# Graph attention: turned one-hots by comparing the edges' rows, queries spread by one fp32 product a chunk

## The chip, the cores and the metric

The kernel runs on one core of one Trainium2 chip. The metric is the device time of one execution in microseconds (us); the time shown for a kernel is the median of its runs. A core has five engines with queues of their own: TensorE (PE) for matrix products, VectorE (DVE), ScalarE (ACT), GpSimd (POOL), and SyncE (SP), which here only issues DMAs. PE keeps one operand of a product still (it is loaded by its own instruction, shown as PEld) [...].

## The reference, cut to what matters

A graph of 3125 nodes with 256 features and 53125 edges (25000 random ones in both directions and a loop at each node, sorted by target node) goes through eight layers in turn: graph attention, a small mixture of experts, a three-layer graph convolution, a second mixture of experts, and so on. Every layer adds its result to `x`. The change is in the first layer, the attention, which computes, for 8 heads of 32 features (`SCALING` is 32 to the power -0.5):

```python
def _L0_gnn_ref(nfeat, attn_bias, Wq, Wk, Wv, Wo, src, dst):    # nfeat = layernorm(x)
    q = (nfeat @ Wq.T).reshape(n, HEADS, HEAD_DIM) / SCALING
    k = (nfeat @ Wk.T).reshape(n, HEADS, HEAD_DIM)
    v = (nfeat @ Wv.T).reshape(n, HEADS, HEAD_DIM)
    attn = jnp.einsum('ehd,ehd->eh', k[src], q[dst])
    attn = attn + attn_bias
    m = jax.ops.segment_max(attn, dst, num_segments=n)
    a = jnp.exp(attn - m[dst])
    s = jax.ops.segment_sum(a, dst, num_segments=n)
    a = a / s[dst]
    out = jax.ops.segment_sum(v[src] * a[:, :, None], dst, num_segments=n)
    return out.reshape(n, FEAT) @ Wo.T
```

So each edge needs the query of its target node (`dst`) and the key and value of its source node (`src`).

## The kernel before, in words

Nodes are cut into T = 25 tiles of P = 125. Since edges are sorted by target, the edges of a tile are one stretch of at most 18 chunks of 128 edges (WC = 18), handled in three parts of PC = 6 chunks. In what follows "tile" is one of the 25.

Setup (`edges_in`, L1735 on) reads the edges by windows, turns them with PE so that an edge has a partition, and leaves `row_w`, the place of each edge's target in its tile, as bf16 (L1755). At the same time keys and values of all nodes are computed and stored to DRAM (`kv_d`), the normalized rows as well (`lt_d`), and the edges' attributes (`eb_d`).

Then comes the loop over tiles. For a tile:

- `one_hot` builds on DVE a matrix `oh` with edges on partitions and a 1 in the column of the edge's target (L282, in bf16); it also issues, on SP, the loads of `lt_t` (L1804) and `eb_t` (L1806).
- `one_hot_turned` transposes `oh` chunk by chunk on PE (L1826, 18 times) and copies the result from PSUM to `oht` by ACT (L1827, three times).
- `queries` computes the tile's queries with two fp32 products (L266, which is the line of the helper `product`) and splits them into three bf16 terms whose sum holds them in full (L1815 to L1819: ACT, DVE, DVE, ACT, DVE in a chain).
- `logits`, once a part, gathers the part's keys and values by POOL's indirect DMAs (`kv`, L1660, six of 256 KB), spreads the queries to the edges by three bf16 products a chunk with `oht` as the still operand (`qx`, L1840), multiplies them into the keys on DVE (L1843, two chunks at a time) and sums per head (L1844). `qx` has two buffers in PSUM.
- `sums_of` makes the exponentials and sums them per target by PE (L1850 to L1858); `weights_of` spreads the sums' logarithms to the edges with `oht` (L1868) and makes the weights.
- `weighted` multiplies the values by the weights (L1878), casts `oh` to fp32 on ACT (L1883) and sums over edges by fp32 products (`acc`, L1885).
- `normed`, `normed_turned` and `projected` divide, transpose (L1902) and multiply by `wo` (L266), and add to `x` (L1909).

The loop is pipelined over three tiles: an iteration computes the logits of tile t (`now`), weights and sums those of tile t-1 (`before`), and prepares tile t+1 (`after`). Between these pieces `beside()` issues one step of the next layer, the experts of two tiles at a time (L770 to L893), and each iteration from the sixth on ends with a step of `Windows` (L1974 on), which prepares a later stage and whose small loads come every fifth tile. The order of the instructions on each engine isn't the order of the text: a planner orders them when the kernel is built, by the order of the text as priority, by its own costs, and by when buffers come free. At run time every engine, and SP's DMA issue, follows that order and waits in it.

Buffers: `kv` has seven, most of the others two. They come from the pool `att_t` (`tiles` in the code), which was laid out before setup's pool.

Of the kernel before, what the change touches and what calls it, by code (L numbers as in the profile page):

```python
# [10 lines left out]
F32 = mybir.dt.float32  # L11
F32R = mybir.dt.float32r
I32 = mybir.dt.int32
BF16 = mybir.dt.bfloat16
AF = mybir.ActivationFunctionType
# [7 lines left out]
N, D = 3125, 256  # L23
# [47 lines left out]
def gnn_ffn_kernel(ctx: ExitStack, tc: tile.TileContext, a, out: bass.AP):  # L71
# [1555 lines left out]
    def attention(windows, experts):  # L1627
# [6 lines left out]
        eb_d = dram.tile([128, T, H, WC], F32, name="eb_d")  # L1634
        win_d = dram.tile([T * WC], I32, name="win_d")
        KO, VO, AO = 16, 16 + D, 7
        WB = T * WC // 5
        with ExitStack() as es:
# [50 lines left out]
            first = big.tile([1, T + 1], F32, name="first")  # L1689
            at = pool.tile([WB, 5], I32, name="win_at", bufs=1)  # L1690

            def begins():
# [42 lines left out]
            def edges_in():  # L1735
# [11 lines left out]
                for ws, to in zip(got, (src_f, dst_f)):  # L1747
                    for b, w in enumerate(ws):
                        wf = pool.tile([WB, 128], F32, name="wf")
                        nc.vector.tensor_copy(wf, w)  # L1750
                        turned(to[:, b * WB:(b + 1) * WB].rearrange("p (t c) -> p t c", t=5), wf)
                    if to is src_f:
                        nc.vector.tensor_copy(src_i, src_f)
                    else:
                        nc.vector.tensor_sub(row_h, twice(dst_f), twice(base.rearrange("p t c -> p (t c)")))  # L1755
                    yield
# [32 lines left out]

            pool = tiles  # L1790
            psum = es.enter_context(tc.tile_pool(name="ps_att", bufs=3, space=PSUM, reuse_waits="tile"))
# [4 lines left out]

            def one_hot(t):
                s = Tile()
                s.t, s.kv = t, begun if t == 0 else []
                oh = pool.tile([128, WC, HC], BF16, name="oh")  # L1800
                one_hots(oh, row_h[:, t * WC:(t + 1) * WC, :], iota_h)
                s.oh = oh[:, :, :P]
                s.lt = pool.tile([128, 2, P], F32, name="lt_t")
                nc.sync.dma_start(s.lt, lt_d[:, :, t, :].rearrange("k f p -> f k p"))  # L1804
                s.eb = pool.tile([128, H, WC], F32, name="eb_t")
                nc.sync.dma_start(s.eb, eb_d[:, t])  # L1806
                return s

            def queries(s):

                ps = psum.tile([P, D], F32, name="sm")
                product(ps, [(s.lt[:, k, :], wq[:, k, :]) for k in range(2)])
                s.q = pool.tile([P, 3, D], BF16, name="q_t")
                q = pool.tile([P, D], F32, name="q")
                nc.scalar.activation(q, ps, AF.Copy, scale=float(HD) ** 0.5)  # L1815
                nc.vector.tensor_copy(s.q[:, 0, :], q)
                nc.vector.tensor_sub(q, q, s.q[:, 0, :])
                nc.scalar.copy(s.q[:, 1, :], q)
                nc.vector.tensor_sub(s.q[:, 2, :], q, s.q[:, 1, :])  # L1819

            def one_hot_turned(s):
                s.oht = pool.tile([P, WC, 128], BF16, name="oht")
                for c0 in range(0, WC, PC):
                    ps = psum.tile([128, 1024], BF16, name="sm")
                    for c in range(PC):
                        nc.tensor.transpose(ps[:P, c * 128:(c + 1) * 128], s.oh[:, c0 + c, :], ident_h)  # L1826
                    nc.scalar.copy(s.oht[:, c0:c0 + PC, :].rearrange("d c e -> d (c e)"),  # L1827
                                   ps[:P, :PC * 128])
                s.l = pool.tile([128, WC, H], F32, name="l")

            def logits(s, p):
# [4 lines left out]
                for c0 in range(0, PC, 2):  # L1836
                    ps = psum.tile([128, 2, D], F32, name="qx", bufs=2)
                    for c in range(2):
                        for k in range(3):
                            nc.tensor.matmul(ps[:, c, :], s.oht[:, p * PC + c0 + c, :], s.q[:, k, :],  # L1840
                                             start=(k == 0), stop=(k == 2))
                    k_ = kv[:, c0:c0 + 2, KO:VO]
                    nc.vector.tensor_mul(k_, k_, ps)  # L1843
# [45 lines left out]
            def normed(s):  # L1889
# [3 lines left out]
                nc.vector.reciprocal(inv, inv)  # L1893
                s.ao = pool.tile([P, D], F32, name="ao")
                nc.vector.tensor_mul(s.ao.rearrange("p (h d) -> p h d", h=H),
# [3 lines left out]
            def normed_turned(s):  # L1899
                ps = psum.tile([128, 2, P], F32, name="sm")  # L1900
                for k in range(2):
                    nc.tensor.transpose(ps[:, k, :], s.ao[:, k * 128:(k + 1) * 128], ident[:P, :P])  # L1902
                s.at = pool.tile([128, 2, P], F32, name="at")
                nc.scalar.copy(s.at, ps)
# [5 lines left out]

            now, before = one_hot(0), None
            one_hot_turned(now)
            queries(now)
            more = experts()
            for t in range(T + 1):
                def beside():
                    more.step(t - 1)

                if now:
                    logits(now, 0)  # L1920
# [5 lines left out]
                beside()  # L1926
                after = one_hot(t + 1) if t + 1 < T else None
                if before:
# [590 lines left out]
```

## Time and profile before

| | us |
|---|---|
| median of 3 runs | 3410.41 |
| lowest, highest | 3407.14, 3412.61 |
| profiled execution, its own time | 3415.6 |
| its span in the profile | 3413.8 |
| first and last qx product | 119.7, 892.4 |
| PE busy | 3132.9 (92%) |
| DVE busy | 1742.2 (51%) |
| ACT busy | 1034.0 (30%) |
| POOL busy | 680.0 (20%) |

The profile is of one execution. Busy time is the time in which at least one instruction of the engine is under way; a matmul's length holds the time that it takes to come out, so the start-to-start distance of several in a row (their pitch) is the better measure of what one costs. "Idle before" is idle time of the engine just ahead of an instruction, and the name behind `<-` is what ended it. The granted clock is the share of TensorE's full clock, as a mean over a stretch. Lines (L1840) are those of the kernel.

### The profile page before, as it was taken

The numbers are of one execution on the slowest core, as the hardware profiler recorded it, in microseconds if no ns is written. First come the engines' busy times: TensorE is split into PE (matmuls) and PEld (weight loads), VectorE is DVE, ScalarE is ACT, GpSimd is POOL, SyncE is SP. The second block draws the span as 40 slices with busy tenths as digits, with TensorE's granted clock in tenths as the row PEclk, the third lists the DMA queues.
The fourth block names the chain that finished last, engine by engine and source line by source line (L and its number), as shares of the span: only waits on it lengthen the run. The fifth ranks groups of instructions, "written<-read, shape, count | busy, mean of one in ns | idle before, by whom it ended". The sixth has DMA issues, their size and how long they took to land. (4 is left out here: it accounts for less than half of the span.)

```text
span 3413.8 us, 45380 instructions
## 1 busy us (share of the span) xinstructions
PE 3132.9 (92%) x16587; PEld 2446.2 (72%) x16587; DVE 1742.2 (51%) x4905; ACT 1034.0 (30%) x1996; POOL 680.0 (20%) x639
## 2 busy tenths in 40 slices
PE   6688998998888899999996999979999999999898
PEld 2466776777677789898885888868755555579666
DVE  6577778777697534344674122155521111355662
ACT  1222332332255423232331222234423232332120
POOL 1665564655100000000134333200000000000000
PEclk9789998999889999999997999989999999999997
DMA  5755554555256734444344666553200000043001
GB/s 165 235 172 150 160 163 143 160 165 144 61 165 215 192 99 119 102 108 110 91 123 133 185 178 180 167 137 103 69 19 10 10 19 10 7 122 100 21 1 39
DMA packets 253208, 388.23 MB, mean 114 GB/s; under 512 B 41454, under 2 KB 201069, under 8 KB 252973
## 3 DMA queue, kind: packets, MB, share of 16 engines
q1 hardware_dynamic: 184090, 226.68, 23.3%
q0 software_dynamic: 54064, 141.25, 15.3%
q10 hardware_dynamic: 14819, 17.27, 1.9%
q8 instruction: 134, 2.20, 0.3%
q14 instruction: 101, 0.83, 0.1%
HBM read 314.47 MB, written 70.58 MB: 113 GB/s over the span
## 5 line engine op out<-in xcount | busy, mean ns | idle before, releaser
L2222 PE MATMUL agg<-cnt_f,hp 125*128 125x500 f32 (+1 forms) x3500 | 733.1, 369 | 22.2 <-ACT hp L2163 22.0
L2222 PEld LDWEIGHTS agg<-cnt_f,hp 125*128 125x128 f32 x3500 | 635.5, 189 | 103.2 <-ACT hp L2163 23.1
L1660 POOL DMA_INDIRECT kv<-kv_d,src_w x450 | 450.9, 1002 | 281.5 <-PE acc L1885 140.5
L2200 ACT CAST cnt_f<-blk 125x500 fp32r<-125x500 bf16 (+1 forms) x435 | 245.5, 565 | 518.4 <-PE agg L2222 496.7
L2200 DVE CAST cnt_f<-blk 125x500 fp32r<-125x500 bf16 (+1 forms) x440 | 185.5, 423 | 265.5 <-PE agg L2222 221.6
L1382 DVE SCALAR_TENSOR_TENSOR x<-po,gall,x 125x256 f32<-125x256 f32 x200 | 93.8, 484 | 417.5 <-PE po L266 416.9
L1376 ACT ACTIVATE h<-hid_ps,shift,scale 128x500 f32<-128x500 f32 (+1 forms) x224 | 161.9, 723 | 376.0 <-PE hid_ps L266 375.5
L1840 PE MATMUL qx<-q_t,oht 125*128 125x256 bf16 x1350 | 216.2, 296 | 53.9 <-DVE kv L1843 41.2
L1885 PE MATMUL acc<-kv,oh_f 128*125 128x265 f32 x900 | 224.9, 412 | 14.6 <-DVE kv L1878 14.6
L1885 PEld LDWEIGHTS acc<-kv,oh_f 128*125 128x125 f32 x900 | 178.5, 201 | 54.2 <-DVE kv L1878 18.5
L1840 PEld LDWEIGHTS <-oht 125*128 125x128 bf16 x1350 | 138.2, 105 | 100.4 <-issue 50.6
L266 PE MATMUL po<-wslot,h 128*125 128x256 f32 x800 | 203.0, 386 | 0.1
L266 PEld LDWEIGHTS po<-wslot,h 128*125 128x125 f32 x800 | 145.0, 187 | 75.2 <-ACT h L1376 27.0
L266 PE MATMUL hid_ps<-h,wslot 128*128 128x500 f32 (+1 forms) x448 | 193.8, 556 | 4.1 <-ACT h L1376 0.6
L266 PE MATMUL hid_ps<-xe,wslot 128*128 128x256 f32 x832 | 187.3, 383 | 1.8 <-DVE xe L1214 1.8
L1072 POOL DMA_INDIRECT xs_d<-r_l,pos x50 | 60.2, 1204 | 645.3 <-DVE r_l L1068 567.1
L266 PE MATMUL hid_ps<-v_rows,wslot 128*128 128x500 f32 (+1 forms) x448 | 186.8, 537 | 0.0
L1225 ACT ACTIVATE hid<-hid_ps,wslot 128x256 f32<-128x256 f32 x208 | 98.5, 475 | 286.8 <-PE hid_ps L266 286.8
L266 PE MATMUL po<-wslot,hid 128*128 128x256 f32 x832 | 184.5, 378 | 0.0
L266 PEld LDWEIGHTS hid_ps<-xe,wslot 128*128 128x128 f32 x832 | 150.7, 191 | 33.4 <-ACT hid L1225 4.1
L266 PEld LDWEIGHTS po<-wslot,hid 128*128 128x128 f32 x832 | 155.7, 189 | 21.8
L1843 DVE TENSOR_TENSOR kv<-kv,qx 128x512 f32<-128x512 f32 x225 | 150.7, 679 | 26.2 <-PE qx L1840 24.7
(512 smaller groups left out, 4625.8 us busy)
## 6 DMA issues: line engine op xcount, KB each, us to landing
wslot<-in_ex_W SPq DMA_DIRECT2D x52, 1024.0 KB
blk<-an_d SPq DMA_DIRECT2D x60, 546.9 KB
blk<-at_d SPq DMA_DIRECT2D x40, 546.9 KB
blk<-an_d SPq DMA_DIRECT2D x45, 410.2 KB
at_d<-ab SPq DMA_DIRECT2D x25, 683.6 KB
an_d<-an SPq DMA_DIRECT2D x25, 683.6 KB
blk<-at_d SPq DMA_DIRECT2D x30, 410.2 KB
kv<-kv_d,src_w POOLq DMA_INDIRECT x450, 3.7
```

The source lines that it names most:

```text
L266: nc.tensor.matmul(ps, l, r, start=(bias is None and i == 0), stop=(i == last))
L1072: st = nc.gpsimd.indirect_dma_start(out=xs_d, in_=l2[:, i, :].bitcast(I32), in_offset=None, out_offset=bass.IndirectOffsetOnAxis(ap=self.p ...
L1225: nc.scalar.activation(hid[:, m, :], ps[:, :BLK], AF.Gelu, bias=c[:, 4 + m:5 + m])
L1376: nc.scalar.activation(dst[:, m, :c], ps[:, :c], AF.Relu, bias=shift[:, l, col:col + 1], scale=scale[:, l, col:col + 1])
L1382: nc.vector.scalar_tensor_tensor(x[:, t0 + i, :], po, gating.all[:, t0 + i, e:e + 1], x[:, t0 + i, :], ALU.mult, ALU.add)
L1660: got = nc.gpsimd.indirect_dma_start(out=kv[:, c, KO:], out_offset=None, in_=kv_d, in_offset=bass.IndirectOffsetOnAxis(ap=src_i[:, at + c: ...
L1840: nc.tensor.matmul(ps[:, c, :], s.oht[:, p * PC + c0 + c, :], s.q[:, k, :], start=(k == 0), stop=(k == 2))
L1843: nc.vector.tensor_mul(k_, k_, ps)
L1885: nc.tensor.matmul(s.acc[:, :D + H + 1], of[:, c, :], kv[:, c, AO:VO], start=(p == 0 and c == 0), stop=(p == 2 and c == PC - 1))
L2200: to(f[:, :n, :], part[0][:, :n, m % MB, :])
L2222: nc.tensor.matmul(ps[f][:, :c], hp[:, m, k, f * 128:(f + 1) * 128], got[:, :c], start=(m == 0 and k == 0), stop=(m == T - 1 and k == 1))
```

## The change

The transposed one-hots are no longer made by transposing. Setup writes the edges' places in their tiles, one row of 128 for each chunk, to a DRAM tensor `turned_d` (five subtractions and five stores). For each tile a load repeats its 18 rows, 4608 bytes, on all 125 partitions; DVE then compares in place with the partition's own number, which gives `oht` directly. The load is issued by a new function `asked`, together with the loads of `lt_t` and `eb_t`, and `asked` for tile t+1 stands at the head of iteration t. ACT casts `oht` to fp32, a part at a time, into `oht_f` with three buffers.

Queries stay in fp32 as they come from PSUM, without the split, and are spread by one fp32 product a chunk.

The tiles of the loop move from `att_t` to a new pool, `att_s`, which is laid out where setup's pool was; `ao` and `at` have one buffer instead of two.

```diff
+        turned_d = dram.tile([T * WC, 128], BF16, name="turned_d")
...
+            first_row = pool.tile([WB, 1], F32, name="first_row", bufs=1)
+            nc.vector.memset(first_row, 0.0)
+            for k in range(1, 5):
+                nc.vector.scalar_tensor_tensor(first_row, pcol[:WB], k * WC - 0.5, first_row, ALU.is_gt, ALU.add)
+            nc.vector.tensor_scalar(first_row, first_row, float(P), None, ALU.mult)
...
+                        if to is dst_f:
+                            wr = pool.tile([WB, 128], BF16, name="wr")
+                            nc.vector.tensor_scalar(wr, wf, first_row, float(b * 5 * P), ALU.subtract, ALU.subtract)
+                            nc.sync.dma_start(turned_d[b * WB:(b + 1) * WB, :], wr)
...
-            pool = tiles
+            pool = es.enter_context(tc.tile_pool(name="att_s", bufs=2, reuse_waits="tile"))
...
-            def one_hot(t):
+            def asked(t):
                 s = Tile()
                 s.t, s.kv = t, begun if t == 0 else []
-                oh = pool.tile([128, WC, HC], BF16, name="oh")
-                one_hots(oh, row_h[:, t * WC:(t + 1) * WC, :], iota_h)
-                s.oh = oh[:, :, :P]
+                s.oht = pool.tile([P, WC, 128], BF16, name="oht")
+                move(nc.sync, s.oht.rearrange("d c e -> d (c e)"), turned_d[t * WC:(t + 1) * WC, :].rearrange("(o c) e -> o (c e)", o=1)
+                     .to_broadcast([P, WC * 128]))
                 s.lt = pool.tile([128, 2, P], F32, name="lt_t")
...
+            def one_hot(s):
+                oh = pool.tile([128, WC, HC], BF16, name="oh")
+                one_hots(oh, row_h[:, s.t * WC:(s.t + 1) * WC, :], iota_h)
+                s.oh = oh[:, :, :P]
...
-                s.q = pool.tile([P, 3, D], BF16, name="q_t")
-                q = pool.tile([P, D], F32, name="q")
-                nc.scalar.activation(q, ps, AF.Copy, scale=float(HD) ** 0.5)
-                nc.vector.tensor_copy(s.q[:, 0, :], q)
-                nc.vector.tensor_sub(q, q, s.q[:, 0, :])
-                nc.scalar.copy(s.q[:, 1, :], q)
-                nc.vector.tensor_sub(s.q[:, 2, :], q, s.q[:, 1, :])
+                s.q = pool.tile([P, D], F32, name="q")
+                nc.scalar.activation(s.q, ps, AF.Copy, scale=float(HD) ** 0.5)
 
             def one_hot_turned(s):
-                s.oht = pool.tile([P, WC, 128], BF16, name="oht")
+                v = s.oht.rearrange("d c e -> d (c e)")
+                nc.vector.tensor_scalar(v, v, pcol[:P], None, ALU.is_equal)
+                s.oht_f = []
                 for c0 in range(0, WC, PC):
-                    ps = psum.tile([128, 1024], BF16, name="sm")
-                    for c in range(PC):
-                        nc.tensor.transpose(ps[:P, c * 128:(c + 1) * 128], s.oh[:, c0 + c, :], ident_h)
-                    nc.scalar.copy(s.oht[:, c0:c0 + PC, :].rearrange("d c e -> d (c e)"),
-                                   ps[:P, :PC * 128])
+                    s.oht_f.append(pool.tile([P, PC, 128], F32, name="oht_f", bufs=3))
+                    nc.scalar.copy(s.oht_f[-1], s.oht[:, c0:c0 + PC, :])
...
-                        for k in range(3):
-                            nc.tensor.matmul(ps[:, c, :], s.oht[:, p * PC + c0 + c, :], s.q[:, k, :],
-                                             start=(k == 0), stop=(k == 2))
+                        nc.tensor.matmul(ps[:, c, :], s.oht_f[p][:, c0 + c, :], s.q, start=True, stop=True)
...
-                s.ao = pool.tile([P, D], F32, name="ao")
+                s.ao = pool.tile([P, D], F32, name="ao", bufs=1)
...
-                s.at = pool.tile([128, 2, P], F32, name="at")
+                s.at = pool.tile([128, 2, P], F32, name="at", bufs=1)
...
-            now, before = one_hot(0), None
+            now, before = asked(0), None
+            one_hot(now)
...
+                after = asked(t + 1) if t + 1 < T else None
                 if now:
                     logits(now, 0)
...
-                after = one_hot(t + 1) if t + 1 < T else None
+                if after:
+                    one_hot(after)
```

## The prediction

> **What bounds the kernel now.** The page first: its groups with their idle times. Columns are busy time, mean length of one, and the idle time of the engine before them with what ended it.
>
> ```profile
> span 3413.8 us, 45380 instructions
> ...
> L1840 PE MATMUL qx<-q_t,oht 125*128 125x256 bf16 x1350 | 216.2, 296 | 53.9 <-DVE kv L1843 41.2
> L1885 PE MATMUL acc<-kv,oh_f 128*125 128x265 f32 x900 | 224.9, 412 | 14.6 <-DVE kv L1878 14.6
> ...
> L1843 DVE TENSOR_TENSOR kv<-kv,qx 128x512 f32<-128x512 f32 x225 | 150.7, 679 | 26.2 <-PE qx L1840 24.7
> ```
>
> The changed products (qx, L1840) are 1350, and their longest idle time is ended by DVE: PE waits there for VectorE's multiply. The view of the qx tile puts them between 119.7 and 892.4 us: 25 tiles, some 31 us each, the only stretch that the change touches but for its setup. Marking it by the first acc product of each tile shows pairs of tiles, because the other work on PE (the experts of two tiles) is spread over two. One pair from 273.9 to 338.4 us, in three parts (busy time by engine, granted clock, DMA share, GB/s), by the view of stages:
>
> ```profile
> 273.90:303.00 29.10, 27.72 (x180) 21.40 (x180) 21.61 (x56) 8.36 (x19) 16.86 (x17) 0.95 0.64 143
> 303.00:320.60 17.60, 17.26 (x91) 13.70 (x92) 11.81 (x22) 6.17 (x10) 13.89 (x12) 1.00 0.57 167
> 320.60:338.40 17.80, 14.14 (x115) 10.64 (x113) 15.60 (x28) 3.98 (x8) 8.80 (x10) 0.80 0.56 165
> ```
>
> Order: PE, PE's weight loads, DVE, ACT, POOL. In the first two parts PE is busy 95 and 98%: it sets the pace. In the third PE has 3.7 us idle, its clock is 0.80, and DVE is busy 88%: VectorE sets it. Who ends PE's waits from 210 to 847 us (ten pairs):
>
> ```profile
> PE qx L1840 <- DVE kv L1843: 25.4, 20, 1.6
> PE acc L1885 <- DVE kv L1878: 8.7, 18, 0.6
> PE qx L1840 <- DVE q_t L1819: 5.7, 9, 0.6
> ...
> PE qx L1840 <- ACT q_t L1818: 1.9, 1, 1.9
> PE sm L266 <- ACT oht L1827: 1.4, 8, 0.2
> ```
>
> Last, PE's timeline of that pair (start, length, count, idle time before) gives pitches:
>
> ```profile
> 283.44 1.21 PE L1826 MATMUL sm<-ident_h,oh 128*125 128x128 bf16 x18
> 288.11 1.02 PE L266 MATMUL sm<-wo,at 128*125 128x256 f32 x4
> 290.20 0.60 PE L1840 MATMUL qx<-q_t,oht 125*128 125x256 bf16 x4 [0.63 <-DVE q_t L1819]
> 298.22 1.36 PE L1840 MATMUL qx<-q_t,oht 125*128 125x256 bf16 x11
> 326.05 0.71 PE L1840 MATMUL qx<-q_t,oht 125*128 125x256 bf16 x5 [1.62 <-DVE kv L1843]
> 331.49 3.38 PE L1840 MATMUL qx<-q_t,oht 125*128 125x256 bf16 x15 [0.55 <-DVE kv L1843]
> ```
>
> With a last matmul of 0.27 us, eleven bf16 products take (1.36 - 0.27)/10 = 0.109 us each. The fp32 product of the same width (projected) is two in the code and four in the trace: an fp32 product is two instructions, (1.02 - 0.38)/3 = 0.213 each. A transpose is (1.21 - 0.22)/17 = 0.058. The last line, 15 products at 0.22, runs at half clock.
>
> [...] The trace shows 0.80 in the part where PE waits most, thus 2 x 0.20 x 17.8 = 7.1 us at half clock[...]. [...] no bf16 tensor_scalar of size is in this trace. [...]
>
> **The change, part by part.**
>
> *Products.* Per chunk 2 x 0.213 = 0.426 for 3 x 0.109 = 0.327: +0.10 us. A pair has 36 chunks: +3.6. The three parts of the pair hold 42, 4 and 62 of its 108 bf16 products, thus 14, 1.3 and 20.7 chunks: +1.4, +0.13, +2.07.
>
> *Transposes* (L1826) go: 18 x 0.058 = 1.05 a tile; one set lies in the first part, one in the second. PE alone would thus gain nothing: +3.6 - 2.1 = +1.5 a pair.
>
> *The split of the queries* goes: two ops of 0.42 and a cast of 0.30 on DVE, a cast of 0.405 on ACT, in a chain DVE, DVE, ACT, DVE. Now q is ready with the scaling copy (0.40 on ACT, kept). The 0.63 wait for q_t in the first part vanishes, so does the 0.18 wait for the copy of the transposes (1.4/8).
>
> *The turned one-hot.* DVE compares 125x2304 bf16 in place. [...] I take 0.81[...]: DVE then has 1.14 - 0.81 = 0.3 less a tile. It stands beside the one_hots (L282) and there DVE idles 0.7 us a tile (12.8 us in 17 waits for ACT), which hides it[...]. ACT: three casts to fp32 of 768, 0.83 each by L1883's 0.818 for 750, for three copies of 0.805: nothing; ACT is a quarter busy. They come in three buffers, each free when the previous tile's products of that part end: those end before the next tile's begin.
>
> *The broadcast.* 125 rows of 4,608 B, 0.58 MB a tile or 18 GB/s on top of some 155 GB/s: DMA share 0.55 to about 0.61. It waits for the buffer of two tiles ago, last read by weights_of (L1868, near 296 and 330 us); the compare comes after the weighting, near 307: 11 us. A gather of 256 KB takes 3.7 us at the median, so I put the landing at 4 to 7 us: hidden. On SP it stands ahead of lt_t and eb_t, which are fetched a tile or more early; behind it also Windows' small loads, every fifth tile, with slack.
>
> *Setup.* Six small DVE ops at 0.15 and five subtractions at 0.275: 2.3 us, DVE being 59% busy there (45.1 of 77 us); five stores on SP, 0.35 each to issue. The new pool lies on setup's memory, so the first loads wait for setup's readers. The first 36 transposes go (114 to 120 us), but 30 bf16 products later PE waits 9.6 us behind DVE, which is held by the experts' weights until 133.3; so nothing earlier is won. Between 0 and +8 us; I take +2. bufs=1 for ao and at costs nothing: each is read before the next tile's is written.
>
> *Sum for a pair.* First part, PE-bound: +1.4 - 1.05 - 0.63 - 0.18 = -0.46. Second, PE-bound: +0.13 - 1.05 = -0.92. Third, DVE-bound: PE's +2.07 fits into its 2.17 us of waits for kv (1.62 + 0.55), so 0; but [...] fewer windows should fall to half clock. At most some 1.6 us are in that, at worst +2.07 are exposed; I take -0.4. Together -1.8 us, 12.5 pairs: -22; with setup -20. The profiled execution of 3413.8 us (3415.6 by its own time) becomes 3394; it lies 3.4 above the median of the runs, 3410.4, which becomes 3390.
>
> **Rivals.**
> 1. *PE sets the third part too* (slower). If the planner's new order leaves DVE waiting for PE, the +2.07 is exposed: -0.46 - 0.92 + 2.07 = +0.7 a pair, +9, with setup +2 to +8: 3424. It decides once more than 1.4 of the 2.07 us show. For it: DVE waits 24.7 us for qx in all, so PE is already last at times. Against: PE waits 41.2 for DVE at the same place.
> 2. *The waits and the half clock go as well* (much faster). PE's 25.4 us of waits for kv fall to a third and the clock goes from 0.95 to 0.99: 17 + 0.04 x 690 = 45 on top: 3345. For it: [...] fp32 fills 0.85 us of every two chunks for 0.65. Against: DVE's own 15.6 of 17.8 us does not shrink.
> 3. *The broadcast lands late* (slower). If it takes more than the 11 us, DVE stops at its compare with the weighting's successors behind it, and PE behind DVE: 2 us a tile, +50: 3440. For it: many reads of one place in DRAM, beside gathers; no run shows one. Against: DMA has 40% free.
>
> **How the numbers follow.** Chances: forecast 0.54 (own range 3370 to 3407), rival 1 0.21, rival 2 0.17, rival 3 0.08. A change of 0.2% (6.8 us) is about what the runs can tell. Faster: 0.47 of the forecast and rival 2, 0.64; same: 0.06 of the forecast and 0.07 of rival 1, 0.13; slower: the rest of rival 1, rival 3 and 0.01 of the forecast, 0.23. The range, 3345 to 3430, reaches to rivals 1 and 2 and leaves out rival 3 and half of rival 2.
>
> **What would show it.** Right: 900 fp32 qx matmuls at 0.21 pitch; no L1826; a pair near 62 us; waits of qx for kv well below 41 us; no wait for q; clock above 0.95 in the stretch. Wrong: DVE's compare waiting for a DMA or lasting over 1.5 us; qx waits as long as before with DVE waiting more for qx (rival 1); attention beginning later than 120 us by more than the setup's share; the planner pulling other work ahead so that acc waits longer for kv (L1878).

## The result and the profile after

| | before | after |
|---|---|---|
| median of 4 runs, us | 3411.51 | 3391.72 |
| lowest, highest | 3407.14, 3413.11 | 3386.11, 3394.98 |
| ratio, 95% interval | | 0.9942 (0.9925 to 0.9960) |
| profiled execution: its own time, span | 3415.6, 3413.8 | 3394.98, 3393.1 |
| first qx product starts, last one ends | 119.65, 892.72 | 126.04, 867.88 |
| last acc product ends | 917.2 | 886.7 |
| next layer's first `hr` | 922.55 | 889.52 |

The kernel became 19.8 us faster, where 20 were predicted (3391.7 against 3390). The way there is another one than predicted, and some of the agreement is two misses that cancel.

The page of the kernel after, span and costliest groups (busy us, mean ns | idle time of the engine before them, what ended most of it):

```profile
span 3393.1 us, 43627 instructions
...
L1849 PE MATMUL qx<-q,oht_f 125*128 125x256 f32 x900 | 243.2, 404 | 8.8 <-DVE kv L1851 5.9
L1893 PE MATMUL acc<-kv,oh_f 128*125 128x265 f32 x900 | 221.9, 398 | 2.9 <-DVE kv L1886 2.4
...
L1851 DVE TENSOR_TENSOR kv<-kv,qx 128x512 f32<-128x512 f32 x225 | 150.2, 680 | 27.3 <-PE qx L1849 23.9
```

There are 900 qx instructions, two for each of the 450 chunks. Their idle time ended by VectorE's multiply (L1851) is 5.9 us, where it was 41.2; for acc it is 2.4, where it was 14.6. All that qx waits is down from 53.9 to 8.8.

Who ends PE's waits after, over the stretch of the qx products (us in total, times, longest):

```profile
PE sm L1864 <- ACT el L1861: 11.0, 12, 1.0
PE sm L1910 <- DVE ao L1903: 6.9, 6, 1.1
PE qx L1849 <- DVE kv L1851: 5.9, 12, 1.9
PE pair L266 <- ACT e L781: 4.7, 1, 4.7
PE pair L266 <- DVE e L779: 4.0, 1, 4.0
```

The waits for the split of the queries are gone: they were 11.2 us in all (5.7 for L1819, 5.5 for L1818), and 0.5 us is left, for the scaling copy ahead of the first product. New waits stand in their place: the sums per target (L1864) wait for the exponentials (11.0 us, 1.6 before), the transposes of `ao` (L1910) for the division, and twice the experts' product `pair` waits 4 to 5 us.

The pair of tiles with three parts, on which the prediction worked, has no counterpart in the pair shown below. PE's timeline after, inside one tile (start, length, count):

```profile
228.60 1.01 PE L266 MATMUL tr<-lt,wslot 128*128 128x250 f32 x4
229.44 1.05 PE L1893 MATMUL acc<-kv,oh_f 128*125 128x265 f32 x4
230.34 1.01 PE L266 MATMUL tr<-s,wslot 128*128 128x250 f32 x4
231.18 1.50 PE L1893 MATMUL acc<-kv,oh_f 128*125 128x265 f32 x6
232.52 1.01 PE L266 MATMUL tr<-lt,wslot 128*128 128x250 f32 x4
```

In this tile the planner puts the 36 acc products in small groups, mostly of four and six, between the experts'. It splits them so in 11 of the 25 tiles, where it split them in 2 before; in the others all 36 stand in a row. The 24 tiles between the first acc products of the first and the last tile take 694.2 us (154.4 to 848.6), where they took 727.0 (150.9 to 877.9): 1.37 us less a tile, 2.7 a pair; 1.8 were predicted. One such pair in the view of stages, cut where the acc products begin (length, then busy PE, PE's weight loads, DVE, ACT, POOL; clock; DMA share; GB/s):

```profile
203.80:228.20 24.40, 22.74 (x121) 18.57 (x122) 19.99 (x47) 7.24 (x15) 19.52 (x17) 0.86 0.71 201
228.20:266.00 37.80, 36.28 (x187) 27.63 (x185) 27.24 (x51) 11.01 (x20) 24.33 (x24) 1.00 0.72 206
```

It takes 62.2 us, with PE busy 93 and 96% and VectorE 82 and 72%: PE sets the pace in all of it, and the VectorE-bound third part is gone.

### The profile page after: what moved, and what is told of

The parts are those of the page before. It is cut to its first block, busy times and chain, and to the rows that moved or that the text cites. A ratio compares the mean times of both kernels' runs of the same rounds, so it can differ in the third digit from the quotient of the medians.

```text
span 3393.1 us, 43627 instructions
## 1 busy us (share of the span) xinstructions
PE 3134.6 (92%) x15687; PEld 2453.3 (72%) x15687; DVE 1730.5 (51%) x4866; ACT 1034.4 (30%) x1973; POOL 699.6 (21%) x639
## 4 chain that ended last, share of the span: by engine, by line
PE 68%; DVE 4%; DMA 2%; issue 2%; ACT 2%; SPq 0%; POOL 0%; ACTq 0%; POOLq 0%; DVEq 0%
PE agg L2233 21%; PE po L266 19%; PE hid_ps L266 15%; PE tr L266 2%; PE acc L1893 2%; PE row L266 1%; PE tok L1536 1%; PE tr L2321 1%; PE tr L250 1%; PE qx L1849 1%; PE bk L2107 1%; DVE hr L282 1%; PE bt L2121 1%; ACT h L1376 1%; PE s L266 0%
## 5 line engine op out<-in xcount | busy, mean ns | idle before, releaser
L1661 POOL DMA_INDIRECT kv<-kv_d,src_w x450 | 471.7, 1048 | 238.4 <-issue 107.8
L1849 PE MATMUL qx<-q,oht_f 125*128 125x256 f32 x900 | 243.2, 404 | 8.8 <-DVE kv L1851 5.9
L1849 PEld LDWEIGHTS qx<-q,oht_f 125*128 125x128 f32 x900 | 171.3, 200 | 43.5 <-DVE kv L1851 14.1
L1851 DVE TENSOR_TENSOR kv<-kv,qx 128x512 f32<-128x512 f32 x225 | 150.2, 680 | 27.3 <-PE qx L1849 23.9
```

Source lines behind the costliest of these rows:

```text
L1661: got = nc.gpsimd.indirect_dma_start(out=kv[:, c, KO:], out_offset=None, in_=kv_d, in_offset=bass.IndirectOffsetOnAxis(ap=src_i[:, at + c: ...
L1849: nc.tensor.matmul(ps[:, c, :], s.oht_f[p][:, c0 + c, :], s.q, start=True, stop=True)
```

## Where the time went in the profiled executions

For each kernel I add up two things between its first and last qx product. *Work* is PE's busy time, with the part that falls into half-clock windows counted half: outside such windows the bf16 products start 0.109 us apart, in one they start 0.22 apart, by the pitches in the prediction. *Lost* is the rest of the stretch: PE's idle time and that other half. Length, busy time and mean clock stand in the same view of stages; the half-clock windows are the trace's record of the granted clock. Before:

```profile
119.65:892.72 773.07, 688.44 (x4517) 534.55 (x4517) 596.05 (x1276) 216.94 (x434) 451.46 (x442) 0.93 0.55 157
```

After:

```profile
126.04:867.88 741.84, 691.99 (x3667) 544.08 (x3668) 584.27 (x1219) 214.72 (x410) 465.75 (x438) 0.96 0.65 181
```

Before, 98.2 of the busy us lie in windows of half clock, so the work is 688.4 - 49.1 = 639.3 and the loss 133.7. After, 61.2 do: the work is 661.4 and the loss 80.5. So PE has 22 us *more* to do, and the stretch is 31 us shorter because 53 us less are lost: PE's idle time falls by 34.8 us (84.6 to 49.9), and the half of its busy time at half clock by 18.5 (49.1 to 30.6).

From there to the end of the kernel: the first product is 6.4 us later; the stretch is 31.2 shorter; from the last product to the next layer's `hr` it is 8.2 shorter (29.8 to 21.6); and from `hr` on, where nothing was changed, the kernel is 12.3 us *longer* (2491.3 to 2503.6). Sum: 6.4 - 31.2 - 8.2 + 12.3 = -20.7, the difference of the spans. In that last part PE is idle for about as long as before (143.1 and 144.0 us), but 127.8 of its busy us are at half clock instead of 109.6. Half of that difference is 9.1 us, the greater part of the 12.3; 0.9 is idle time, and the other 2.4 are busy time that this sum doesn't explain. That this part starts 33 us earlier (889.52 against 922.55) may have to do with it; no run shows that. In the four other kernels that were profiled where the kernel before takes 3412 us, the same unchanged part took 2494.0 to 2499.5 us, so it moves by several us from one kernel to the next.

## The experiments

Eight kernels were run, some of them more than once: twelve runs in three sets of four, each set beside its own runs of the kernel before. The three sets met different conditions: the kernel before took 3412, 3772 and 3800 us in them. Below, "the first condition" is the one in which it takes 3412 us, as it did when the change was measured. Ratios are comparable within a set; the two halves of the change were run in all three conditions.

### One half of the change at a time

*Compare alone*: `oht` is compared as after, the queries are split and spread as before. Against the kernel after:

```diff
-                s.q = pool.tile([P, D], F32, name="q")
-                nc.scalar.activation(s.q, ps, AF.Copy, scale=float(HD) ** 0.5)
+                s.q = pool.tile([P, 3, D], BF16, name="q_t")
+                q = pool.tile([P, D], F32, name="q")
+                nc.scalar.activation(q, ps, AF.Copy, scale=float(HD) ** 0.5)
+                nc.vector.tensor_copy(s.q[:, 0, :], q)
...
-                    s.oht_f.append(pool.tile([P, PC, 128], F32, name="oht_f", bufs=3))
-                    nc.scalar.copy(s.oht_f[-1], s.oht[:, c0:c0 + PC, :])
...
-                        nc.tensor.matmul(ps[:, c, :], s.oht_f[p][:, c0 + c, :], s.q, start=True, stop=True)
+                        for k in range(3):
+                            nc.tensor.matmul(ps[:, c, :], s.oht[:, p * PC + c0 + c, :], s.q[:, k, :],
+                                             start=(k == 0), stop=(k == 2))
```

> One half of the change alone: one-hots turned by the compare, queries still split and spread by three bf16 products. Theory of the prediction: the 18 transposes (1.05 us a tile of PE) go, 26 us in all; the compare adds 0.8 us of VectorE a tile, of which up to 0.4 may show in the part that VectorE sets (10 us); the later start, 6.4 us in the changed kernel, stays: 10 to 20 us faster than before, 3392 to 3402, waits of qx for kv at some 40 us as before. Rival (the fp32 products took the waits away, not the transposes): no more than 5 us faster, 3406 to 3415, and about 110 us at half clock as before.

> Compared one-hots alone, with the three bf16 products and the split, once more, for a chip on which the kernel before takes 3411 us. There the theory (transposes and the wait for their copy go from PE-bound parts, 1.05 a tile, less the late start of 6 us) expects 10 to 20 us less than before, ratio 0.994 to 0.997; the rival (that the products' own waits for VectorE and the half clock fall because of the fp32 products) expects no more than 0.997 here. On a chip with 3770 to 3800 us before: 0.9725 to 0.978 again.

*fp32 alone*: the product and the unsplit queries as after, `oht` by transposes on PE and copies as before, then cast to `oht_f`. Against the kernel after:

```diff
-                s.oht = pool.tile([P, WC, 128], BF16, name="oht")
-                move(nc.sync, s.oht.rearrange("d c e -> d (c e)"), turned_d[t * WC:(t + 1) * WC, :].rearrange("(o c) e -> o (c e)", o=1)
-                     .to_broadcast([P, WC * 128]))
...
-                v = s.oht.rearrange("d c e -> d (c e)")
-                nc.vector.tensor_scalar(v, v, pcol[:P], None, ALU.is_equal)
+                s.oht = pool.tile([P, WC, 128], BF16, name="oht")
+                for c0 in range(0, WC, PC):
+                    ps = psum.tile([128, 1024], BF16, name="sm")
+                    for c in range(PC):
+                        nc.tensor.transpose(ps[:P, c * 128:(c + 1) * 128], s.oh[:, c0 + c, :], ident_h)
+                    nc.scalar.copy(s.oht[:, c0:c0 + PC, :].rearrange("d c e -> d (c e)"),
+                                   ps[:P, :PC * 128])
```

> The other half alone: transposes by PE kept (ACT copies them out and casts them to fp32 as well), queries in fp32, one fp32 product a chunk. Theory of the prediction: +3.6 us of PE a pair, 2.1 of them hidden, the waits for the split gone (0.63): +0.9 a pair, so 5 to 15 us slower than before, 3416 to 3426. Rival (fp32 products took the waits away): waits of qx for kv fall from 41 us to below 15, half clock falls by 40 us, and the kernel is 5 to 20 us faster, 3390 to 3405.

> fp32 products alone, with the transposes on PE, once more, for a chip on which the kernel before takes 3411 us. The theory (products cost PE +0.10 us a chunk, of which the VectorE-bound third part hides more than half, the split's wait of 0.63 a pair goes) expects between 5 us less and 15 us more than before, ratio 0.9985 to 1.004; the rival (PE's waits for the multiply into the keys fall with the number of products, and the half clock with them) expects 10 to 20 us less, 0.994 to 0.997. On a chip with 3770 to 3800 us before: 0.994 again.

Measured, in the first condition (before 3412.11, 25 runs):

| | median us | ratio (95%) | against before |
|---|---|---|---|
| compare alone | 3413.33 | 1.0009 (1.0001 to 1.0017) | +1 |
| fp32 alone | 3439.66 | 1.0085 (1.0068 to 1.0101) | +28 |
| both (the kernel after, own set) | 3391.72 | 0.9942 (0.9925 to 0.9960) | -20 |

No half gains anything, together they gain 20 us. The halves add up to +29, so 49 us are in their meeting. The theory falls for both halves. The rival, that the fp32 products take the waits away and not the transposes, has the time of compare alone right (3406 to 3415) and that of fp32 alone wrong (3390 to 3405). The views of stages, of compare alone:

```profile
126.56:882.70 756.14, 661.19 (x4101) 507.27 (x4101) 602.64 (x1291) 167.32 (x363) 465.21 (x438) 0.93 0.63 178
```

and of fp32 alone:

```profile
123.77:917.79 794.02, 721.72 (x4081) 571.46 (x4081) 581.50 (x1195) 262.04 (x482) 435.76 (x440) 0.95 0.53 152
```

| between first and last qx, us | length | PE busy | of it at half clock | work | lost | idle, of what is lost |
|---|---|---|---|---|---|---|
| before | 773.1 | 688.4 | 98.2 | 639.3 | 133.7 | 84.6 |
| compare alone | 756.1 | 661.2 | 95.3 | 613.5 | 142.6 | 95.0 |
| fp32 alone | 794.0 | 721.7 | 67.6 | 687.9 | 106.1 | 72.3 |
| after | 741.8 | 692.0 | 61.2 | 661.4 | 80.5 | 49.9 |
| after, transposes too (below) | 749.6 | 698.9 | 22.1 | 687.9 | 61.7 | 50.7 |

The column *work* is just what the prices say. 450 transposes at 0.058 us are 26.1 us, and compare alone has 25.8 less. 450 chunks at 0.426 - 0.327 are 44.6, and fp32 alone has 48.6 more. After has 22.1 more, where 44.6 - 26.1 = 18.5. The column *lost* is what no price foretold. (The profiled execution of compare alone took 3405.6 us, 8 less than its median, so its row is somewhat flattering.)

What the fp32 products do shows in PE's waits of fp32 alone:

```profile
PE tr L770 <- DVE g L735: 26.0, 9, 3.2
PE qx L1851 <- DVE kv L1853: 3.7, 3, 1.3
```

The second line is the wait for VectorE's multiply. It is 41.2 us before and 23.5 in compare alone, but 3.7 here, 5.9 in the kernel after, and 5.0 in the kernel with the transposes put back below. Of the 41.2, one wait at the start is 9.6; without the start, from 154 to 848 us, the five are 28.7, 19.6, 1.1, 2.8 and 2.2. So the wait is small in the three kernels that have the fp32 products, and not in the two that don't. Busy time at half clock goes the same way (98.2 and 95.3 us without them, 67.6, 61.2 and 22.1 with them). This much of the rival's mechanism came as it said. The small groups of acc products aren't the reason: compare alone has them too, in 11 tiles, and fp32 alone in none. That an fp32 product, being longer, gives VectorE more time for each chunk (0.426 us for 0.327, by the pitches) is the likely reason, but it is argued.

Yet the fp32 products put 48.6 us of work on PE and take only 27.6 from what is lost. The largest wait that is left is the first line; PE's timeline at one of the nine places:

```profile
281.93 1.13 PE L266 MATMUL sm<-wq,lt_t 128*125 128x256 f32 x4 [0.19 <-ACT oht L1835]
282.90 0.38 PE L1912 MATMUL sm<-ident,ao 125*128 125x125 f32 x2
286.11 0.58 PE L770 MATMUL tr<-ident,g 125*4 125x125 f32 x2 [2.83 <-DVE g L735]
286.48 1.07 PE L1851 MATMUL qx<-q,oht_f 125*128 125x256 f32 x2
```

The transpose of the experts' gates (L770) stands on PE ahead of qx products, while VectorE, in a chain of small ops, has them only at 286.06. In the attention the kernel before has no wait of L770 for L735, and the kernel after one of 0.14 us. PE stands still for 2.8 us or more at nine places where the planner put this transpose too early. The 26.0 us are near what this kernel is slower than the one before, but that is no account of it: the account is 48.6 of work less 27.6.

In compare alone, qx still waits 23.5 us for VectorE's multiply, and the sums wait 19.9 for the exponentials, where that was 1.6 before:

```profile
PE qx L1851 <- DVE kv L1854: 23.5, 27, 3.3
PE sm L1867 <- ACT el L1864: 19.9, 15, 1.4
```

### The transposes put back, off the chain

The kernel after, with the transposes and their copies issued as well, into a tile that nobody reads:

```diff
                     nc.scalar.copy(s.oht_f[-1], s.oht[:, c0:c0 + PC, :])
+                    ps = psum.tile([128, 1024], BF16, name="sm")
+                    for c in range(PC):
+                        nc.tensor.transpose(ps[:P, c * 128:(c + 1) * 128], s.oh[:, c0 + c, :], ident_h)
+                    spare = pool.tile([P, PC * 128], BF16, name="spare", bufs=1)
+                    nc.scalar.copy(spare, ps[:P, :PC * 128])
```

> The kernel after, with the 18 transposes of each tile issued on PE again, and the three bf16 copies from PSUM on ACT, into a scratch tile that nobody reads: work is added back, the chain through it is not, and the result stays the reference's. If the gain of the compared one-hots is PE's own time for the transposes, 25 x 1.05 = 26 us come back where the kernel before takes 3411 us (a ratio of 0.994 + 0.008 = 1.002), and some 60 to 100 us where it takes 3770 to 3800 (a ratio of 0.99 to 1.0). If the gain is that the products no longer wait for a chain from DVE over PE and ACT, and that the planner orders the work otherwise, less than 10 us come back on the first kind of chip and less than 25 us on the second (a ratio below 0.98).

Measured: 3398.18 us, ratio 0.9960 (0.9947 to 0.9972). That is 6.5 us more than the kernel after, not 26; the difference is one between sets, and the two intervals overlap. Its view of stages:

```profile
125.78:875.36 749.58, 698.91 (x4081) 554.85 (x4081) 589.68 (x1219) 268.19 (x482) 459.06 (x439) 0.99 0.63 179
```

PE does 26.5 us more than after (687.9 against 661.4), and loses 18.8 less (61.7 against 80.5). The transposes don't fill idle time, which is 49.9 us without them and 50.7 with them. It is the clock that pays: the mean rises from 0.96 to 0.99, and the half of the busy time at half clock falls from 30.6 to 11.0. So taking 26 us of transposes off PE isn't worth 26 us here.

The best comparison is with fp32 alone. Both kernels do the same work on PE, 4081 matmul records and 687.9 us, transposes and fp32 products alike. They differ in what the products wait for (a compare, or transposes, copy and cast in a chain), in the broadcast, and in the order. The one takes 3398.2, the other 3439.7: 41 us for the same PE work. In the stretch, fp32 alone loses 44.4 us more: 21.6 of idle time and 22.7 of half clock. Its 26.0 us at L735 don't occur in this kernel's list at all, and that is more than the whole difference in idle time. So what the compare brings to the whole change is not PE's own time for the transposes. The standstills at L735, which the planner's order decides, are the largest part of it that the traces show; that the half clock follows from them is argued. That the products wait for that chain itself isn't shown: in fp32 alone PE waits only 1.7 us for the copies of the turned one-hots, and no qx product for their cast. A kernel with the old order and the new chain can't be had by an edit, since the planner follows both.

### The late start and the late broadcast

In the kernel after, SP's queue around one iteration that contains a step of Windows:

```profile
284.57 0.31 SPq L107 DMA_DIRECT2D oht<-turned_d  x1
288.53 0.26 SPq L2032 DMA_DIRECT2D win_p<-ptr_d  x1
288.84 1.26 SPq L108 DMA_DIRECT2D oht<-turned_d  x1
```

VectorE's compare, and then PE, behind it:

```profile
298.19 0.82 DVE L1834 TENSOR_SCALAR oht<-oht,pcol 125x2304 bf16<-125x2304 bf16 x1 [5.59 <-DMA oht<-turned_d]
```

```profile
300.30 1.09 PE L266 MATMUL pair<-e,wslot 128*64 128x250 f32 x2 [4.71 <-ACT e L781]
```

The broadcast goes out in two pieces, of 112 and 13 partitions. Between them SP waits for Windows' store of its pointers to land, to load them again (L2032); the second piece leaves at 288.84 and VectorE's compare starts 9.4 us later. VectorE waits 5.6 us for it, and PE 4.7 for a step of ScalarE that stands behind a cast of the compare's result. At 607.6 it happens again (4.4 and 3.95 us).

*Both mended*: the turned one-hots and the queries' rows take memory from the old pool, and Windows' load moves to its next step.

```diff
-                s.oht = pool.tile([P, WC, 128], BF16, name="oht")
+                s.oht = tiles.tile([P, WC, 128], BF16, name="oht")
...
-                s.lt = pool.tile([128, 2, P], F32, name="lt_t")
+                s.lt = tiles.tile([128, 2, P], F32, name="lt_t")
...
-                at = pool.tile([P, 1], I32, name="win_p", bufs=1)
-                nc.sync.dma_start(at, ptr_d.rearrange("(q o) -> q o", o=1))
                 if t0 + n == T:
...
                 yield
+                at = pool.tile([P, 1], I32, name="win_p", bufs=1)
+                nc.sync.dma_start(at, ptr_d.rearrange("(q o) -> q o", o=1))
```

> The kernel after with two edits: the turned one-hots and the rows of the queries take their memory from the old pool, so that the first loads need not wait for setup's memory, and Windows' load of its pointers is issued a step later, so that it does not hold the broadcast behind a store that is still landing. If the late start (first product 6.4 us later) comes from the pool, the first product comes back to about 120 us, and 3 to 6 us are won; if it comes from the edges' attributes' stores ahead of it on SP, nothing is. The waits of VectorE's compare for the broadcast (10.6 us in 3 places) should go, with PE's waits of 4.7 and 4.0 us behind them: 3 to 8 us. Together 3 to 14 us below the kernel after: a ratio to before of 0.990 to 0.9935 where before takes 3411 us, 0.968 to 0.972 where it takes 3770 to 3800. The rival, that these waits lie in slack, expects the ratio of the kernel after.

Measured: 3379.24 us, ratio 0.9898 (0.9868 to 0.9929). It beats both kernels: 33 us below before, and some 12 below after, though that last difference is one between sets, whose intervals still touch. The start, on PE of the kernel after:

```profile
123.52 2.04 PE L266 MATMUL sm<-wq,lt_t 128*125 128x256 f32 x4 [12.00 <-issue]
126.04 6.26 PE L1849 MATMUL qx<-q,oht_f 125*128 125x256 f32 x20 [0.47 <-ACT q L1830]
134.16 3.04 PE L1849 MATMUL qx<-q,oht_f 125*128 125x256 f32 x12 [1.87 <-DVE kv L1851]
```

and of the mended one:

```profile
117.37 2.76 PE L1849 MATMUL qx<-q,oht_f 125*128 125x256 f32 x8
120.32 3.04 PE L1849 MATMUL qx<-q,oht_f 125*128 125x256 f32 x12 [0.19 <-DVE kv L1851]
134.24 8.32 PE L1849 MATMUL qx<-q,oht_f 125*128 125x256 f32 x24 [10.87 <-DVE kv L1851]
```

The pool was the cause of the late start: the first product is at 117.4 again. But PE then waits 10.9 us for VectorE, as it did before the change (9.6), and both kernels are at about the same product near 134. By the first acc product 2.1 us are left of 8.7 (152.3 against 154.4). The prediction's sentence that nothing earlier is won at this place holds to 2 us.

The broadcast: SP's queue and the compare in the mended kernel.

```profile
281.67 0.31 SPq L107 DMA_DIRECT2D oht<-turned_d  x1
282.04 0.39 SPq L108 DMA_DIRECT2D oht<-turned_d  x1
285.90 0.26 SPq L2036 DMA_DIRECT2D win_p<-ptr_d  x1
```

```profile
293.12 0.82 DVE L1834 TENSOR_SCALAR oht<-oht,pcol 125x2304 bf16<-125x2304 bf16 x1 [3.43 <-DMA oht<-turned_d]
```

Both pieces are out together and still the compare has to wait, until 11.1 us after the second. So only part of the lateness was the queue; the rest is how long this load takes. By its packets in the trace, the last one ends 10.6 us after the first piece's issue; at the median of the 25 tiles it is 5.8. VectorE's wait goes from 5.6 to 3.4 here, PE's two waits at `pair` from 8.7 to 4.6 us. The expectation that they go was wrong. By the last acc product the mended kernel is 6.5 us ahead (880.2 against 886.7), of which 2.1 + 4.1 are these two; the other 4 us of the 10.7 between the two spans come after the attention, where nothing differs, and I can't tell them from the several us by which that part moves between kernels, as seen above (2494.0 to 2499.5).

### The sets in the other conditions

In the second set (before 3771.91), besides both halves:

*The pool alone* (the kernel before; `att_s`, and one buffer for `ao` and `at`):

```diff
-            pool = tiles
+            pool = es.enter_context(tc.tile_pool(name="att_s", bufs=2, reuse_waits="tile"))
...
-                s.ao = pool.tile([P, D], F32, name="ao")
+                s.ao = pool.tile([P, D], F32, name="ao", bufs=1)
...
```

> The kernel before, with its tiles in the new pool on setup's memory and with one buffer for ao and at; nothing else. Theory: only the start moves, since the first loads wait for setup's memory; 0 to 6 us slower, 3411 to 3418, and the stretch from the first to the last acc as long as before (766 us). Rival (the later start of the changed kernel comes from its load of the turned rows, which has to pass SP's queue): no change within 2 us, the first qx at 120 us.

*The split's chain taken away* (the kernel before; it leaves out the second and third term of the queries, and spreads the first three times):

```diff
-                s.q = pool.tile([P, 3, D], BF16, name="q_t")
-                q = pool.tile([P, D], F32, name="q")
-                nc.scalar.activation(q, ps, AF.Copy, scale=float(HD) ** 0.5)
-                nc.vector.tensor_copy(s.q[:, 0, :], q)
...
+                s.q = pool.tile([P, D], BF16, name="q_t")
+                nc.scalar.activation(s.q, ps, AF.Copy, scale=float(HD) ** 0.5)
```

> The kernel before without the split of the queries: they are rounded to one bf16 term, and the three products spread that one term three times, so the output leaves out the two smaller terms and holds the largest thrice. PE's work is that of before; two subtractions and a cast on VectorE and a cast on ACT go. Theory: the wait of 0.63 us a pair goes and what VectorE saves lies where it isn't the bound: 8 to 12 us faster, 3399 to 3404. Rival (VectorE's saving shortens the part it sets): 1.1 us a tile, some 25 us faster, 3386.

In the third set (before 3800.01), besides both halves again, the kernel after itself and *Windows' load later* (the last of the edits above, alone):

> The changed kernel itself, unaltered. In the first four runs the kernel before took 3772 us, against 3411 when the change was measured; its engines stood still for up to 8 us again and again in the attention, with nothing to wait for. If this run finds before at some 3411, the ratio should be 0.994 as measured; if it finds 3772, the ratio tells what the change does where that other cause is at work, and both theories leave it open: 0.97 if the compare's gain of 2.2% there stands in the whole change, 0.99 if not.

> Compare-made one-hots with the three bf16 products, again. If before takes some 3411: the prediction's theory 3392 to 3402; the rival (the fp32 products took the waits away) 3406 to 3415, with some 110 us at half clock. If before takes 3772: 0.978 again.

> PE's transposes with fp32 queries and products, again. If before takes some 3411: the prediction's theory 3416 to 3426; the rival 3390 to 3405 with waits of qx for kv below 15 us. If before takes 3772: 0.994 again.

> The changed kernel with one DMA issued later: Windows' load of win_p, which waits on SP for a store to land (16.8 us in four times in the changed kernel's trace) and holds the broadcast behind it, moves to the next step. Theory: VectorE's waits for the broadcast (10.6 us in three) fall below 3, PE's two waits of 4.7 and 4.0 us go: 6 to 10 us faster than the changed kernel, ratio to before 0.2% to 0.3% below that of the changed kernel in the same call. Rival (those waits are slack of PE and come back elsewhere): no difference to it beyond 2 us.

| | before there | median us | ratio (95%) |
|---|---|---|---|
| compare alone | 3771.91 | 3688.82 | 0.9781 (0.9755 to 0.9806) |
| fp32 alone | 3771.91 | 3747.66 | 0.9937 (0.9914 to 0.9960) |
| the pool alone | 3771.91 | 3777.28 | 1.0014 (1.0004 to 1.0023) |
| no split chain | 3771.91 | 3783.56 | 1.0033 (1.0023 to 1.0043) |
| the kernel after | 3800.01 | 3697.74 | 0.9726 (0.9699 to 0.9752) |
| compare alone | 3800.01 | 3701.88 | 0.9725 (0.9693 to 0.9757) |
| fp32 alone | 3800.01 | 3778.26 | 0.9942 (0.9914 to 0.9971) |
| Windows' load later | 3800.01 | 3698.74 | 0.9722 (0.9691 to 0.9753) |

What can be taken from these: the pool costs 5 us by itself (1.5 to 8.7 by the interval), inside the 0 to 8 that the prediction gave setup and pool together. Removing the split's chain alone, with VectorE's and ScalarE's work, gained nothing; it made the kernel 12 us slower. And Windows' load, moved alone, gained nothing that shows against the kernel after. All three were in the other conditions, though. There the compare alone brings the whole gain, and five times as much of it; in the first condition it brings none. So what one half is worth can't be carried from one condition to another.

What is different there shows by the same sum. The kernel of the pool alone has 1083.5 us between its first and last qx product, with 639.7 of work, the very work of the kernel before (639.3). Lost are 443.8 instead of 133.7. The kernel after has 665.1 of work there (661.4 in its own set) and loses 382.4. Standstills like this one, in the timeline of PE of the pool alone, do it:

```profile
421.27 0.60 PE L1840 MATMUL qx<-q_t,oht 125*128 125x256 bf16 x4
428.86 1.22 PE L266 MATMUL tr<-wslot,s 128*125 128x256 f32 x2 [6.99 <-issue]
```

Seven us pass in which PE waits for nothing that the profile shows. In the traces of the first condition PE has none of over 1 us between the first and the last qx product (ahead of the first, at the late start, the kernel after has one of 12.0 us). What causes it stays open. The sets at 3412 and at 3772 us bear the same number of the chip in the record, that at 3800 another, so that number alone doesn't decide it. The rest of the kernel, from the last acc product on, takes as long as elsewhere (3759.6 - 1260.1 = 2499.5, against 2496.6 for the kernel before).

## Why the prediction was right in its number, and where not

*The prices were right.* The compare takes 0.812 us at the median, where 0.81 was taken; that was the author's estimate, and the trace before has no operation to show it. The cast takes 0.828 (0.83), and PE's work rises by 22 us where the fp32 products and the transposes were to make it 18.5 more. VectorE has 11.8 us less to do in the stretch, 0.47 a tile; 0.3 were estimated.

*"PE's +2.07 fits into its 2.17 us of waits for kv", and "I take -0.4"* (half clock). The prediction claimed 22 us less in the stretch with 18.5 more work, that is, 41 us less lost. It was 53. The direction of both terms was right. But the first size comes from an order that no longer exists, and the -0.4 was the author's estimate, with no run behind it. The planner made a new order, in which qx's waits for VectorE fall by 35 of 41 us (26 of 29 without the start), and PE's busy time at half clock by 37 us (98.2 to 61.2), which is 18.5 us of time or 1.5 a pair instead of 0.4. Against that stand 16.3 us more of waits for exponentials and division (11.0 and 6.9, where it was 1.6 and none) and 8.7 at `pair`. So rival 2 is half true: both its terms came, with 26 us of waits without the start where it said 17, and 18.5 of clock where it said 28, and then a part was given back.

*The sum over parts.* The prediction gave each part its own worth: transposes and their copy, -2.3 us a pair, should have gained some 28 us alone, less the setup; fp32 products should have cost little alone (+3.6 - 0.63 - 2.07 - 0.4 = +0.5 a pair, 6 us). Measured, they are +1 and +28. This is the step that fails: in a kernel whose instructions are ordered anew for every edit, with PE's idle and half-clock time of 134 us in reach, an edit's worth is not its work. The transposes put back cost only some 6.5 of their 26 us, because the clock paid for the rest; the fp32 products alone bring 48.6 us of work and 26.0 of standstill at a place that the prediction doesn't name. That the sum came out right for both together is luck as much as insight.

*Setup, "I take +2"*. It was 6.4 at the first product, inside the bound of 8; a start later than 120 us by more than setup's share was one of the prediction's own signs of being wrong. The pool was the reason named, and the mended kernel shows it.

*"Hidden", and Windows' loads "with slack".* The 4 to 7 us for the landing were right for most tiles: by its packets in the trace, the load's last one ends 5.8 us after the first issue at the median, and within 4 to 7 us in 18 of 25 tiles. But six loads take longer, up to 12.6 us, and the 11 us of slack aren't there: where VectorE doesn't wait, the compare stands 6.8 to 10.7 us behind the issue. SP's wait for the pointers' store, up to 6.9 us, comes in four iterations, between the broadcast's pieces in three and ahead of them in one; in two of the four VectorE then waits. It waits 13.1 us in all for the load, in five tiles, and PE 8.7 behind it in two. That is rival 3, at two tiles instead of all.

*Rival 1* didn't come: PE sets more of the pace, as it said, but the waits that went were more than the work that came.

*After the attention the prediction counted nothing.* It was +12.3 us, 9.1 of them half clock. Together with the late start this hides that the attention itself gained 39 us (31.2 + 8.2), not 22.

## What to carry to other kernels

Split a stretch that one engine bounds into the work at full clock and the lost time, idle and half clock together: the first can be priced to a few us from pitches, the second has to be measured, since with a planner it belongs to the whole order and not to the edit. Where much is lost, taking work away may gain nothing (25.8 us of transposes: +1) and adding it may cost a quarter of its length (26.5 us of them: 6.5). Look in the new order both for the waits that went and for those that came, before you put a gain down to the work removed. Check two halves of a change together as well as apart before you drop the one that loses by itself.

## What the runs showed of the hardware that was not expected

- The clock rose when PE was given more to do: with 26 us of transposes added to it, the stretch went from 0.96 to 0.99, half-clock time from 64.5 to 22.1 us (one execution of each). The half-clock stretches last 3.4 us or a multiple of it, up to 41 us, but for the one in which the trace ends (38 of 39 in the trace before, 35 of 36 after). PE wasn't idle ahead of them: before the change, between the first and the last qx product, it was busy for 57% of the 3.4 us ahead of such a stretch at the median, and for 42 to 86% at the extremes, against 89% of the whole stretch.
- In the kernel after, a broadcast of 4608 B to 125 partitions (0.58 MB) beside gathers has its last packet 5.8 us after its issue at the median, 3.2 to 12.6 at the extremes, with packets of 262 ns at the mean.
- The same kernel took 3412, 3772 and 3800 us in three sets. The work on PE between the first and the last qx product was the same to 4 us (639.3 and 639.7 with the old products, 661.4 and 665.1 for the kernel after). What differed is the time lost there, and for part of the standstills the profile names no releaser.
